# An adaLN block on one core: the work before the first scores in another order, modulation rows through SyncE's queue, x one group further ahead, slot scatters four and four, and k's two passes set between the halves of q's scaling

## Chip, core and metric

One Trainium2 chip, of which one core is used. The core has five engines with a queue of instructions each: PE (TensorE, with PEld for its weight loads), DVE (VectorE), ACT (ScalarE), POOL (GpSimd) and SP (SyncE, which only starts transfers). An engine takes its instructions in order and waits for semaphores of the others. Transfers (DMAs) are started by ACT, POOL or SP and then run by themselves. The metric is the device time of one execution in microseconds, as the median of several; smaller is better.

## What is computed

An adaptive-layernorm transformer block over 4 sequences of 2048 tokens of width 256, all in float32:

```python
mod = (silu(c) @ wmod).reshape(4, 6, 1, 256)
sa, ca, ga, sb, cb, gb = (mod[:, i] for i in range(6))
ga = (2*(ga >= 0) - 1) * maximum(abs(ga), 0.25)      # gb likewise
h = layernorm(x) * (1 + ca) + sa
x = x + ga * attention(h, w_qkv, w_out)
h = layernorm(x) * (1 + cb) + sb
x = x + gb * moe(h, w_router, w_gate, w_down)
```

The attention is causal and linear: 16 heads of 16 numbers, phi = elu + 1 on q and k, a running sum S of k v^T and z of k, out = (q S) / max(q z, 1e-6). The expert stage routes each token to 2 of 8 experts by a softmax, with a capacity of 1280 tokens an expert in the order of the tokens; all experts share the gate matrix (silu(h w_gate)) and have their own down matrix. The two weighted results are added.

## The kernel before

**Tiling.** 8192 tokens make 16 groups of 512, and a group is 4 tiles of 128. Four groups are one sequence. The kernel has two stages. The first (until about 640 us) does everything up to the routed rows, group by group; the second runs the experts over 8 × 1280 slots and adds to the output. The second stage is the same in both kernels.

**First stage.** Inside a chunk of 128 tokens the attention is done with a masked 128 × 128 score matrix per head, and across chunks with a running state. Step s of the main loop (from L876) is tile j = s mod 4 of group g = s div 4. Each step does the scores of its tile (psc, L482; masked into at, L488), the attention of the tile before (po, L545 and L558), its state and its output product (project_out, L572: pw in L576, added to x by DVE in L577, followed by the statistics of the second norm, L316). Between them stand pieces of other groups:
- g+3: load_x (L83, at j = 1, through SP) and sums (L268, row sums on ACT, at j = 3).
- g+2: deviations (L289, squares on ACT, then ve, rstd and nmr on POOL), normalise (L334, ACT), to_features (L343: transposes pta and a scaled copy hTa), and at j = 3 the two halves of k (project, L359: product pk on PE, exp into exk and relu into k on ACT; finish_keys adds them on DVE in L380 later).
- g+1: at j = 0 the two halves of q (pq, the same project), running_keys (L415: zc, a running sum of k on DVE, and qs = zc × q on POOL in L428, one half of the heads at j = 0, the other at j = 1), keys_by_token (L401: transposes of k, copied to kk), values (L382: pv, copied to vpad), denominators (L430: pd on PE, den in L441 and rden in L443 on DVE), scaled_q (L447: pr on PE, qs on DVE in L461), and at j = 3 heads_apart (L466: four scaled copies qeo on ACT).
- g−1: second norm (hrow), transposes ptm, logits (pl, L615; turned to tokens as lt, L628), ranks (L630, at j = 3), scale_rows (L596: hrow × modr on POOL in L600) and, in the next group, shift_rows (hrow + modr on DVE in L606).
- g−2: positions (L678: counts turned into places, pp), dispatch (L690: some fifteen small DVE operations L706 to L728 that make slot numbers) and send (L739): eight indirect scatters on POOL that write a group's rows into the table slots in DRAM. They are issued three at j = 2, three at j = 3 and two at j = 0 of the next group.

The order within PE, ACT, DVE and POOL is the order in which the program calls these functions. That on SP is chosen by the framework under the dependencies. In ranks, DVE takes a maximum and a difference (L644, L646), ACT the exp (gates, L647), DVE the sum sm (L649) and nine more operations to mask (L665), and POOL adds mask up into cnt (L674).

**PSUM.** pq, pk, pv, pg, pd, pw, lt, pp and the transposes take turns on three banks (pool ps); a product waits until the content of its bank has been read. Scores and po have their own.

**Lead-in.** Before the loop (L842 to L872) the pieces for group 0 and some of group 1 are called in one stretch. modulation_rows (L214) multiplies c by the columns of wmod for ga, gb (first pg), cb and sb (second pg), forms the rows on DVE (sgn, neg, then mod_rows), and sends them by ACT's queue to DRAM (mod_d, L239) and back, copied to all partitions, one transfer a sequence (modr, L241). modr's ga row is first used by gated_out (L566, POOL: wob = wout × ga), which project_out needs; its cb and sb rows by the second norm; hrow takes the gb row from mod_d (L590). constants_last (L152) sets constants of the routing. free_slots(i, then) (L731) fills one tenth of slots with a row of an unused place, by 8 SP transfers of 262 KB, and starts after the operation given. All ten must be written before the first scatter.

**x.** xpool holds 4 groups of x: load_x takes a buffer when the group it held has been written out.

Of the kernel before, what the change touches and what calls it, by code (L numbers as in the profile page):

```python
# [48 lines left out]
G = 512  # L49
NT = G // P  # L50
GPB = L // G
NH = D // P
# [14 lines left out]
def adaln_block(ctx: ExitStack, tc, x, wqkvT, woutT, wrT, wgT, wdT, cT, wmod, out):  # L67
# [3 lines left out]
    const = ctx.enter_context(tc.tile_pool(name="const", bufs=1))  # L71
    ps = ctx.enter_context(tc.tile_pool(name="ps", bufs=3, space=PSUM))
    tokens = ctx.enter_context(ExitStack())
    xpool = tokens.enter_context(tc.tile_pool(name="xpool", bufs=4))

    def bank(name):
        return ps.tile([P, 512], F32, tag="bank", name=name)
# [133 lines left out]
                modc[:, at + i].rearrange("p h b -> p (h b)"), pc[:, i * n : (i + 1) * n], float(i), None, ALU.add  # L211
            )

    def modulation_rows():  # L214

        rows_ = sp.tile([NB, 4, D], F32, name="mod_rows")
        sgn = sp.tile([NB, 2 * D], F32, name="sgn")
        neg = sp.tile([NB, 2 * D], F32, name="neg")
        for i, pair in enumerate(((2, 5), (4, 3))):
            pg = bank(f"pg_{i}")  # L220
            for n, m in enumerate(pair):
                for k in range(NH):
                    nc.tensor.matmul(
                        pg[:NB, n * D : (n + 1) * D], sc[:, k, :], wmod_sb[:, k, m * D : (m + 1) * D],
                        start=(k == 0), stop=(k == NH - 1),
                    )
            if i == 1:
                nc.vector.tensor_scalar(rows_[:, 1, :], pg[:NB, :D], 1.0, None, ALU.add)
                nc.vector.tensor_copy(rows_[:, 2, :], pg[:NB, D:])
                continue  # L230

            nc.vector.tensor_scalar(sgn, pg[:NB, :], 0.0, 2.0, ALU.is_ge, ALU.mult)
            nc.vector.tensor_scalar(neg, pg[:NB, :], -1.0, 0.25, ALU.mult, ALU.max)
            nc.vector.tensor_tensor(neg, neg, pg[:NB, :], ALU.max)  # L234
            nc.vector.scalar_tensor_tensor(
                rows_[:, 0::3, :], sgn.rearrange("b (a d) -> b a d", d=D), -1.0,
                neg.rearrange("b (a d) -> b a d", d=D), ALU.add, ALU.mult,
            )
        nc.scalar.dma_start(mod_d[:, :, :], rows_)  # L239
        for b in range(NB):  # L240
            nc.scalar.dma_start(modr[:, b], mod_d[b : b + 1, :3, :].to_broadcast([P, 3, D]))  # L241

    def token_rows():
        setup.close()
# [156 lines left out]
    def keys_by_token(g):  # L401
        kT = G_["k", g]
        kk = G_["kk", g] = w2.tile([P, NT, NH, P], F32, tag="kk", name=f"kk_{g}")
        for j in range(0, NT, 2):
            pk = bank(f"pk_{g}_{j}")
            for i in range(2):
                for h in range(NH):
                    nc.tensor.transpose(
                        pk[:, (i * NH + h) * P : (i * NH + h + 1) * P],
                        kT[:, h, (j + i) * P : (j + i + 1) * P],  # L410
                        ident,
                    )
            nc.scalar.copy(kk[:, j : j + 2].rearrange("p j h s -> p (j h s)"), pk)

    def running_keys(g, hs):  # L415

# [46 lines left out]
                pr[:, :, h, 0, :], ALU.mult,  # L463
            )

    def heads_apart(g):  # L466

        qs = G_["qs", g]
        qeo = G_["qeo", g] = w2.tile([P, NH, 2, G], F32, tag="qeo", name=f"qeo_{g}")
        for h in range(NH):  # L470
            for q in range(2):
                nc.scalar.activation(qeo[:, h, q, :], qs[:, h, :], AF.Copy, scale=par[:, q : q + 1])

# [360 lines left out]
    with tc.manual_schedule(engines={ET.PE, ET.Activation, ET.DVE, ET.Pool}):  # L834
# [35 lines left out]
        gated_out(0)  # L870
        free_slots(2, project(1, "k", 0, D, 2))
        sums(2)  # L872

        out_bank("po_first")
        last = None
        for s in range(NG * NT + 1):  # L876
# [28 lines left out]
            if tail:  # L905
# [1 line left out]
                p15a, p15b, p15c = (NG - 1, 0, 2), (NG - 1, 2, 1), (NG - 1, 3, 1)  # L907
                t = s - (NG - 1) * NT
                if t == 0:
                    send((NG - 4, 0, NT), 6, 8)  # L910
                    shift_rows(p13)
                    positions(p13)
                    done()
# [50 lines left out]
                    dispatch(p15c)  # L964
                    send(p15c, 0, 2)
            if old is not None and j in (2, 3):
                send(old, 3 * (j - 2), 3 * (j - 1))
            if s == 0:
                free_slots(3, project(1, "k", 1, D, 2))
            elif s == 2:  # L970
                modulation_columns((3, 4), 2)
                token_rows()
            if tail:
                pass
            elif j == 0:
# [8 lines left out]
                    deviations(g - 1 if prv is not None else None, nrm)  # L984
                if nxt is not None:
                    running_keys(nxt, (0,))
                if g >= 3:
                    send((g - 3, 0, NT), 6, 8)
                if old is not None:
                    shift_rows(old)  # L990
            elif j == 1:
                if nxt is not None:
                    keys_by_token(nxt)
                done()
                if old is not None:
                    positions(old)
                if nxt is not None:
                    running_keys(nxt, (1,))
                    values(nxt, 0)
                    values(nxt, 2)  # L1000
                if nrm is not None:
                    normalise((nrm, 0, NT), "a", xs[nrm], G_["xna", nrm])
                if old is not None:
                    dispatch(old)
                if far is not None:
                    load_x(far)
            elif j == 2:
                if nxt is not None:
                    denominators(nxt)
                if prv is not None:  # L1010
                    second_norm(prv)
                if nrm is not None:
                    to_features((nrm, 0, NT), "a", 0)
                done()
                if nxt is not None:
                    scaled_q(nxt)
                if prv is not None:
                    to_features(prv, "m", 2)
            else:
# [84 lines left out]
```

## Time and profile before

| | us |
|---|---|
| runs of the kernel | 948.67, 950.0, 952.56 (median 950.0) |
| profiled execution | 952.95 |
| its span, first to last instruction | 951.2 |
| busy PE / DVE / POOL / ACT | 839.8 / 553.2 / 488.5 / 417.1 |
| mean granted TensorE clock | 0.951 of full |
| first stage / second stage | about 640 / 311 |
| first scores of group 0, 1, 2, 3, 4 | 51.39, 83.34, 114.60, 156.39, 190.5 |

The last row is read from the timeline: the difference of two entries is what a group takes. In the rows of a timeline, the first number is the start in us from the span's start, the second the length of the instruction or of a run of equal ones (x and a count). Then come the engine (a q behind it means that the engine starts a transfer), the line, the operation, and output <- inputs with their shapes. A bracket gives how long the engine had stood idle before, and who ended that wait. In a table of stretches each row has the stretch, its length, the busy time of each engine with the number of instructions, the granted TensorE clock, the share of time that the transfer engines worked, and GB/s.

The two instructions with the most DVE and POOL time in the first stage are these (busy time, mean ns of one, then idle time before them): 

```profile
L488 DVE TENSOR_TENSOR at<-psc,tri 128x1024 f32<-128x1024 f32 x128 | 150.2, 1214 | 27.8 <-PE psc L482 27.8
L745 POOL DMA_INDIRECT slots<-hrow,idx x128 | 137.6, 1075 | 49.8 <-issue 35.2
```

### The profile page before, as it was taken

What the parts mean: (1) busy time and instruction counts of PE and PEld (TensorE: products, weight loads), DVE (VectorE), ACT (ScalarE), POOL (GpSimd) and SP (SyncE); (2) the same over time, 40 slices, a digit from 0 to 9 for tenths busy, and PEclk for the clock granted to TensorE, in tenths of its full rate; (3) what the DMA queues carried; (4) which work ended last, traced back from release to release, by engine and by line L of the source; (5) the groups of instructions that cost most, each with busy time, mean ns of one, the idle gap of its engine ahead of it and who ended that gap; (6) DMA issues with size and microseconds to landing.
All of it is one profiled execution on the core that took longest, in us unless ns stands there. A gap on an engine that the chain in (4) does not pass through costs nothing.

```text
span 951.2 us, 20608 instructions
## 1 busy us (share of the span) xinstructions
PE 839.8 (88%) x8234; PEld 583.2 (61%) x8234; DVE 553.2 (58%) x1193; ACT 417.1 (44%) x973; POOL 488.5 (51%) x607
## 2 busy tenths in 40 slices
PE   6599979899899889889889887628999999999995
PEld 3366656666566566566566564415767767767664
DVE  3456676797697697687687687752333333333332
ACT  3355555566566655656656533112222222222220
POOL 1321344765765676675676567651434434434334
PEclk9689999999999999999999988758999999999999
DMA  7578903313322322321221111029546546645333
GB/s 272 197 249 235 326 29 106 122 50 127 115 85 102 114 92 85 121 91 45 80 81 52 50 41 43 1 67 305 102 101 151 130 101 127 148 102 106 34 36 42
DMA packets 72217, 106.16 MB, mean 112 GB/s; under 512 B 9251, under 2 KB 44323, under 8 KB 72121
## 3 DMA queue, kind: packets, MB, share of 16 engines
q1 hardware_dynamic: 44192, 65.22, 21.4%
q0 software_dynamic: 21760, 31.99, 15.5%
q10 hardware_dynamic: 6168, 7.63, 2.3%
q8 instruction: 65, 1.06, 0.5%
q14 instruction: 32, 0.25, 0.1%
HBM read 42.97 MB, written 74.69 MB: 124 GB/s over the span
## 4 chain that ended last, share of the span: by engine, by line
PE 49%; POOL 13%; DVE 12%; issue 7%; ACT 4%; DMA 1%; POOLq 0%; another core or an unknown queue 0%; DVEq 0%; ACTq 0%; SPq 0%
PE ph L796 13%; PE pe L809 13%; PE pk L366 5%; POOL slots L745 4%; PE pw L576 3%; DVE at L488 3%; PE psc L482 2%; PE ptm L352 2%; POOL rstd L306 2%; PE pq L366 2%; PE po L558 2%; POOL qs L428 2%; PE pte L785 2%; POOL out_dram L818 1%; PE po L545 1%
## 5 line engine op out<-in xcount | busy, mean ns | idle before, releaser
L818 POOL DMA_INDIRECT out_dram<-y,tok x80 | 123.3, 1541 | 180.3 <-DVE y L814 126.4
L488 DVE TENSOR_TENSOR at<-psc,tri 128x1024 f32<-128x1024 f32 x128 | 150.2, 1214 | 27.8 <-PE psc L482 27.8
L745 POOL DMA_INDIRECT slots<-hrow,idx x128 | 137.6, 1075 | 49.8 <-issue 35.2
L796 PE MATMUL ph<-hTe,wg_sb 128*128 128x512 f32 (+1 forms) x384 | 153.1, 526 | 0.0
L809 PE MATMUL pe<-wd,hid 128*128 128x256 f32 x640 | 150.5, 379 | 0.0
L809 PEld LDWEIGHTS pe<-wd,hid 128*128 128x128 f32 x640 | 121.6, 190 | 37.0 <-issue 23.0
L802 DVE SCALAR_TENSOR_TENSOR hid<-th,ph 128x512 f32<-128x512 f32 (+1 forms) x96 | 57.4, 598 | 145.8 <-ACT th L801 140.8
L801 ACT ACTIVATE th<-ph 128x512 f32<-128x512 f32 (+1 forms) x96 | 50.5, 526 | 156.1 <-PE ph L796 153.8
L796 PEld LDWEIGHTS ph<-hTe,wg_sb 128*128 128x128 f32 x384 | 70.3, 193 | 39.0 <-issue 32.5
L482 PE MATMUL psc<-qeo,k 32*128 32x256 f32 x1024 | 75.8, 410 | 10.5 <-PE po L545 4.1
L366 PE MATMUL pk<-hTa,wqkv_sb 128*128 128x512 f32 x128 | 67.0, 649 | 6.7 <-DVE x L577 6.2
L576 PE MATMUL pw<-wob,both 128*128 128x256 f32 x236 | 65.9, 404 | 7.7 <-ACT both L513 5.4
L558 PE MATMUL po<-at,vpad 128*32 128x128 f32 x2048 | 70.8, 277 | 0.7 <-issue 0.6
L814 DVE SCALAR_TENSOR_TENSOR y<-pe,rows 128x256 f32<-128x256 f32 x80 | 38.7, 484 | 49.7 <-PE pe L809 49.7
L482 PEld LDWEIGHTS psc<-qeo,k 32*128 32x128 f32 x1024 | 48.4, 190 | 30.0 <-issue 9.4
L558 PEld LDWEIGHTS po<-at,vpad 128*32 128x32 f32 x2048 | 54.1, 110 | 18.5 <-issue 18.1
L366 PE MATMUL pq<-hTa,wqkv_sb 128*128 128x512 f32 x128 | 62.6, 614 | 0.0
L388 PE MATMUL pv<-wqkv_sb,hTa 128*128 128x256 f32 x256 | 59.9, 387 | 1.8 <-DVE neg L234 1.8
L576 PEld LDWEIGHTS pw<-wob,both 128*128 128x128 f32 x236 | 43.4, 200 | 24.2 <-issue 11.2
L788 ACT COPY hTe<-pte 128x512 f32<-128x512 f32 (+1 forms) x48 | 24.7, 514 | 69.2 <-PE pte L785 69.1
L674 POOL TENSOR_TENSOR cnt<-cnt,mask 128x8 f32<-128x8 f32 x56 | 19.5, 347 | 68.9 <-DVE mask L665 65.6
L388 PEld LDWEIGHTS pv<-wqkv_sb,hTa 128*128 128x128 f32 x256 | 47.9, 191 | 8.4 <-issue 2.3
(163 smaller groups left out, 1358.0 us busy)
## 6 DMA issues: line engine op xcount, KB each, us to landing
slots<-free SPq DMA_DIRECT2D x80, 262.0 KB, 5.2
rows<-slots SPq DMA_DIRECT2D x16, 1048.0 KB, 8.3
x<-in_x_dram SPq DMA_DIRECT2D x16, 512.0 KB
out_dram<-x SPq DMA_DIRECT2D x16, 512.0 KB, 5.6
rows<-slots SPq DMA_DIRECT2D x8, 524.0 KB, 3.6
hrow<-mod_d SPq DMA_DIRECT2D x32, 128.0 KB, 3.0
wd<-in_wdT_dram ACTq DMA_DIRECT2D x8, 512.0 KB
slots<-hrow,idx POOLq DMA_INDIRECT x128
```

Source lines behind the costliest of these rows:

```text
L366: nc.tensor.matmul(pq, wqkv_sb[:, k, o + h * P : o + (h + 1) * P], hT[:, k, :], start=(k == 0), stop=(k == NH - 1))
L388: nc.tensor.matmul(pv[:, i * D : (i + 1) * D], hT[:, k, (j + i) * P : (j + i + 1) * P], wqkv_sb[:, k, 2 * D : 3 * D], start=(k == 0), stop ...
L482: nc.tensor.matmul(psc[:, a, h], kT[r : r + 32, h, cols], qeo[r : r + 32, h, :, cols], start=True, stop=True,)
L488: masked = nc.vector.tensor_tensor(at, psc[:, 2 * m : 2 * m + 2].rearrange("p i h q t -> p (i h q) t"), tri.unsqueeze(1).to_broadcast([P, ...
L558: nc.tensor.matmul(po[32 * a : 32 * a + 32, h * P : (h + 1) * P], vp[:, j, h * 4 + a, q : q + 2, :], att[a // 2][:, a % 2, h, q, :], start ...
L576: nc.tensor.matmul(pw[:, :D], oT[:, h, :], wob[:, h, :], start=(h == 0), stop=(h == NH - 1))
L745: row = nc.gpsimd.indirect_dma_start(out=slots[:, :], out_offset=bass.IndirectOffsetOnAxis(ap=idx[:, c, j : j + 1], axis=0), in_=hr[:, j0 ...
L796: nc.tensor.matmul(ph[:, :m], wg_sb[:, k, f * P : (f + 1) * P], hTs[b][:, k, :m], start=(k == 0), stop=(k == NH - 1),)
L801: nc.scalar.activation(th[:, :m], ph[:, :m], AF.Tanh, scale=0.5)
L802: nc.vector.scalar_tensor_tensor(hids[b][:, f, :m], th[:, :m], 1.0, ph[:, :m], ALU.add, ALU.mult)
L809: nc.tensor.matmul(pe[:, :D], hids[b][:, f, j * P : (j + 1) * P], wds[e][:, f, :], start=(f == 0), stop=(f == NF - 1),)
L818: put = nc.gpsimd.indirect_dma_start(out=out[:, :], out_offset=bass.IndirectOffsetOnAxis(ap=toks[b][:, j : j + 1], axis=0), in_=y, in_offs ...
```

## The change

It has five parts.

1. **modulation_rows** becomes row_products, gate_rows and norm_rows. The rows go to mod_d in three transfers and come back in eight (four ga rows, four pairs of cb and sb rows), all by SP. In the lead-in the first half of pg stays after values(0, 0); constants_last, normalise(1) and the denominators, values, scaled_q and heads_apart of group 0 come in front of the rest; the second half of pg comes late. k's first pass and the sums that stood at the lead-in's end, and two of the slot fills, move behind the scores of step 0; gated_out(0) moves to step 0, behind running_keys(1, (0,)), which on POOL is the first half of group 1's qs.
2. **x**: five buffers, and at j = 1 of group g group g+4 is loaded, not g+3. x_3 is loaded at step 0.
3. **Scatters**: four at j = 2, four at j = 3, none at j = 0.
4. **k's passes**: at j = 3 ACT scales one half of q's heads, then does k's first pass, then scales the other half.
5. **ranks** is called in front of the output product of j = 3 and of k's second pass, not behind them.

On SP the order becomes x_0, wqkv, x_1, wg, x_2, x_3, x_4; 8 slot writes; 3 writes of mod_d; 8 broadcasts into modr; 64 slot writes; out of group 0; 8 slot writes; the 8 first gb rows of hrow; x_5. Before, it is x_0, wqkv, x_1, wg, x_2, x_3; 56 slot writes; 6 gb rows; 8 slot writes; 2 gb rows; 8 slot writes; out of group 0; 8 slot writes; x_4.

```diff
-    xpool = tokens.enter_context(tc.tile_pool(name="xpool", bufs=4))
+    xpool = tokens.enter_context(tc.tile_pool(name="xpool", bufs=5))
...
-    def modulation_rows():
+    mod_rows = sp.tile([NB, 4, D], F32, name="mod_rows")
+    def row_products(i, pair):
+        pg = bank(f"pg_{i}")
...
+        return pg
+    def gate_rows(pg):
...
-        nc.scalar.dma_start(mod_d[:, :, :], rows_)
+        for i in (0, 3):
+            nc.sync.dma_start(mod_d[:, i, :], mod_rows[:, i, :])
         for b in range(NB):
-            nc.scalar.dma_start(modr[:, b], mod_d[b : b + 1, :3, :].to_broadcast([P, 3, D]))
+            nc.sync.dma_start(modr[:, b, 0, :], mod_d[b : b + 1, 0, :].to_broadcast([P, D]))
+    def norm_rows(pg):
+        nc.vector.tensor_scalar(mod_rows[:, 1, :], pg[:NB, :D], 1.0, None, ALU.add)
+        nc.vector.tensor_copy(mod_rows[:, 2, :], pg[:NB, D:])
+        nc.sync.dma_start(mod_d[:, 1:3, :], mod_rows[:, 1:3, :])
+        for b in range(NB):
+            nc.sync.dma_start(modr[:, b, 1:3, :], mod_d[b : b + 1, 1:3, :].to_broadcast([P, 2, D]))
...
-    def heads_apart(g):
+    def heads_apart(g, hs=tuple(range(NH))):
...
         values(0, 0)
-        modulation_rows()
-        free_slots(1, denominators(0))
+        gates = row_products(0, (2, 5))
+        constants_last()
+        normalise((1, 0, NT), "a", xs[1], G_["xna", 1])
+        denominators(0)
         values(0, 2)
-        normalise((1, 0, NT), "a", xs[1], G_["xna", 1])
         scaled_q(0)
         heads_apart(0)
+        gate_rows(gates)
         to_features((1, 0, NT), "a", 0)
-        keys_by_token(0)
-        constants_last()
-        gated_out(0)
-        free_slots(2, project(1, "k", 0, D, 2))
-        sums(2)
+        norm_rows(row_products(1, (4, 3)))
+        free_slots(1, keys_by_token(0))
...
                 if t == 0:
-                    send((NG - 4, 0, NT), 6, 8)
...
             if old is not None and j in (2, 3):
-                send(old, 3 * (j - 2), 3 * (j - 1))
+                send(old, 4 * (j - 2), 4 * (j - 1))
             if s == 0:
+                free_slots(2, project(1, "k", 0, D, 2))
                 free_slots(3, project(1, "k", 1, D, 2))
+                sums(2)
+                load_x(3)
...
-                if g >= 3:
-                    send((g - 3, 0, NT), 6, 8)
                 if old is not None:
                     shift_rows(old)
+                if g == 0:
+                    gated_out(0)
...
-                if far is not None:
-                    load_x(far)
+                if g + 4 < NG:
+                    load_x(g + 4)
...
                 if nxt is not None:
-                    heads_apart(nxt)
+                    heads_apart(nxt, (0,))
                 if nrm is not None:
                     project(nrm, "k", 0, D, 2, later=True)
+                if nxt is not None:
+                    heads_apart(nxt, (1,))
                 if prv is not None:
                     logits_by_token(prv)
+                    ranks(prv)
                 done()
                 if nrm is not None:
                     project(nrm, "k", 1, D, 2, later=True)
-                if prv is not None:
-                    ranks(prv)
```

More of the change, by code (lines that the diff above doesn't have):

```diff
@@ L212, in modulation_columns @@
             )
-    def modulation_rows():
-        rows_ = sp.tile([NB, 4, D], F32, name="mod_rows")
+    mod_rows = sp.tile([NB, 4, D], F32, name="mod_rows")
+    def row_products(i, pair):
+        pg = bank(f"pg_{i}")
+        for n, m in enumerate(pair):
+            for k in range(NH):
+                nc.tensor.matmul(
+                    pg[:NB, n * D : (n + 1) * D], sc[:, k, :], wmod_sb[:, k, m * D : (m + 1) * D],
+                    start=(k == 0), stop=(k == NH - 1),
+                )
+        return pg
@@ L217, in modulation_rows @@
+    def gate_rows(pg):
         sgn = sp.tile([NB, 2 * D], F32, name="sgn")
         neg = sp.tile([NB, 2 * D], F32, name="neg")
[L219 to L238, printed above, removed]
@@ L239, in modulation_rows @@
-        nc.scalar.dma_start(mod_d[:, :, :], rows_)
-        for b in range(NB):
-            nc.scalar.dma_start(modr[:, b], mod_d[b : b + 1, :3, :].to_broadcast([P, 3, D]))
+        nc.vector.tensor_scalar(sgn, pg[:NB, :], 0.0, 2.0, ALU.is_ge, ALU.mult)
+        nc.vector.tensor_scalar(neg, pg[:NB, :], -1.0, 0.25, ALU.mult, ALU.max)
+        nc.vector.tensor_tensor(neg, neg, pg[:NB, :], ALU.max)
+        nc.vector.scalar_tensor_tensor(
+            mod_rows[:, 0::3, :], sgn.rearrange("b (a d) -> b a d", d=D), -1.0,
+            neg.rearrange("b (a d) -> b a d", d=D), ALU.add, ALU.mult,
+        )
@@ L412, in keys_by_token @@
                     )
-            nc.scalar.copy(kk[:, j : j + 2].rearrange("p j h s -> p (j h s)"), pk)
+            inst = nc.scalar.copy(kk[:, j : j + 2].rearrange("p j h s -> p (j h s)"), pk)
+        return inst
     def running_keys(g, hs):
@@ L464, in scaled_q @@
             )
-    def heads_apart(g):
+    def heads_apart(g, hs=tuple(range(NH))):
         qs = G_["qs", g]
-        qeo = G_["qeo", g] = w2.tile([P, NH, 2, G], F32, tag="qeo", name=f"qeo_{g}")
-        for h in range(NH):
+        if 0 in hs:
+            G_["qeo", g] = w2.tile([P, NH, 2, G], F32, tag="qeo", name=f"qeo_{g}")
+        qeo = G_["qeo", g]
+        for h in hs:
             for q in range(2):
```

## The prediction

> **What bounds the kernel now.** I read the page first. TensorE is busy 88% of the span, but the chain that ended last gives it only 49%; VectorE and GpSimd hold 12 to 13% each, so in places another engine sets the pace. The expert stage (640 to 951 us) has 295.5 us of TensorE work in 311 and no edit touches it. All that can move lies before. There I took the timelines engine by engine, the chain of waits, and tables by stretch.
>
> *Lead-in.* The first scores (psc) start at 51.39 us. In ScalarE's and TensorE's timelines:
>
> ```profile
> 32.04 0.52 ACTq L239 DMA_DIRECT2D mod_d<-mod_rows  x1
> 33.80 7.31 ACTq L241 DMA_DIRECT2D modr<-mod_d  x4
> 41.15 0.65 ACT L396 COPY vpad<-pv 128x256 f32<-128x256 f32 x2 [15.62 <-DMA modr<-mod_d]
> ...
> 42.35 2.79 PE L352 MATMUL pta<-ident,xna 128*128 128x128 f32 x8 [7.74 <-ACT xna L339]
> ```
>
> ScalarE stands still for 15.62 us in front of a copy whose product (pv, second half) was ready at 33.4, and normalise(1), which TensorE waits 7.74 us for, stands behind that copy.
>
> *Group 2, once.* x_4 is asked for at 115.12, behind the last slot write:
>
> ```profile
> 115.12 0.38 SPq L85 DMA_DIRECT2D x<-in_x_dram  x1
> ...
> 121.45 0.42 ACT L273 ACTIVATE xna<-x 128x256 f32<-128x256 f32 x1 [6.11 <-DMA x<-in_x_dram]
> ...
> 123.51 1.57 PE L576 MATMUL pw<-wob,both 128*128 128x256 f32 x4 [4.72 <-ACT both L513]
> 124.88 3.18 PE L366 MATMUL pq<-hTa,wqkv_sb 128*128 128x512 f32 x4
> ```
>
> The stretches by start of a group's scores (length, then busy of PE, PEld, DVE, ACT, POOL; clock; DMA) show the price and the steady period:
>
> ```profile
> 114.60:156.40 41.80, 34.44 (x451) 23.39 (x447) 27.76 (x56) 21.43 (x54) 20.04 (x29) 0.92 0.28 94
> 156.40:190.50 34.10, 31.24 (x433) 21.62 (x429) 26.73 (x56) 21.40 (x54) 22.05 (x29) 1.00 0.28 103
> 261.30:295.70 34.40, 31.52 (x448) 21.88 (x449) 26.79 (x56) 21.56 (x54) 22.72 (x31) 1.00 0.32 106
> ```
>
> *Steady state.* A period is 34.4 us with only 31.5 of TensorE. What holds it, at the end of a group (ScalarE, VectorE, TensorE):
>
> ```profile
> 290.25 2.56 ACT L472 ACTIVATE qeo<-qs,par 128x512 f32<-128x512 f32 x4
> 292.71 0.58 ACT L370 ACTIVATE exk<-pk 128x512 f32<-128x512 f32 x1
> 293.19 0.59 ACT L371 ACTIVATE k<-pk 128x512 f32<-128x512 f32 x1
> 295.22 0.60 ACT L370 ACTIVATE exk<-pk 128x512 f32<-128x512 f32 x1 [1.45 <-PE pk L366]
> ...
> 296.19 0.23 ACT L647 ACTIVATE gates<-gates 128x32 f32<-128x32 f32 x1
> ...
> 296.45 0.18 DVE L649 TENSOR_REDUCE sm<-gates 128x4 f32<-128x32 f32 x1 [2.53 <-ACT gates L647]
> ...
> 293.20 1.98 PE L366 MATMUL pk<-hTa,wqkv_sb 128*128 128x512 f32 x4 [0.52 <-DVE x L577]
> ```
>
> and earlier in it (TensorE, GpSimd):
>
> ```profile
> 281.62 0.42 PE L436 MATMUL pd<-qs,hpick 128*32 128x128 f32 x8 [1.25 <-POOL qs L428]
> ...
> 276.49 1.82 POOL L745 DMA_INDIRECT slots<-hrow,idx  x1 [0.17 <-issue]
> 278.62 0.97 POOL L745 DMA_INDIRECT slots<-hrow,idx  x1 [0.30 <-issue]
> ```
>
> From the gates' arrival (sm, 539.90) to pr (562.53) the chain of waits is 22.6 us of almost nothing but VectorE, back to back; the 11.8 us left of a period are TensorE and ScalarE up to the next gates. Two things tie for that stretch's end: this VectorE queue (rden after den) and GpSimd's qs, late behind two scatters. Removing one of the two alone gives next to nothing.
>
> **The change part by part.**
>
> *1. Lead-in.* Off ScalarE go the issues (0.52 + 7.31) and the two waits between them. [...] The row says 15.62: ScalarE's queue stays in order over a wait for the rows and one for their write. I take the row, because compute stands behind those waits, and rebuild the stretch. pg's first half (8 of 16 matmuls, half of 3.78) ends at 26.7; pd 29.0 as before; den and rden 1.2 → 30.3; second half of v to 30.9, pr 1.24 → 32.1; qs 2 × 0.6 → 33.3. ScalarE: normalise(1) 30.85 to 32.9, vpad → 33.6, qeo 2.56 → 36.1. VectorE's gate rows free pg's bank at 35.3, the other half of pg runs 35.3 to 37.1, eight transposes of k 1.1 → **38.2**, or 40.1 at half clock (the granted clock was 0.50 between 34 and 52 us). But k's first pass of group 1 (3.6 us before the first scores until now) moves behind them; at psc(0,1), where both orders have done the same, I get 47.0 to 48.9 against 58.54: 9.6 to 11.5 us, 9.6 taken.
>
> A new wait: gated_out(0) moves on GpSimd behind group 1's rstd, nmr and first qs (1.7 + 0.2 + 1.3 and their inputs). The output product pw(0,0) needs its wob: some 7.6 us after psc(0,1) where TensorE is there after 3.6, so −4.0. Queued behind pw on TensorE is all of the next step. Below: nothing, if TensorE is late itself; above: 5.7, if half clock follows (x_4's wait made pq 3.18 for 1.88). Net **−5.5** (−3.5 to −7.5).
>
> SP: its 11 modulation DMAs stand behind 8 slot writes and in front of 64. The rows land near 43, first used by group 0's second norm, far later. The 64 then run from 43.5; at 0.83 each (6.61 for 8 at 99.94) to 97, eight more and the gb rows to about 108. The first scatter is near 129. At the worst row (9.99 for 8) they end near 138, and first scatters and x_5 would lose up to 9.
>
> *2. x ahead.* x_4 is seventh on SP, in front of every slot write, so the 6.11 goes. In TensorE: 4.72 idle + (3.18 − 1.88) + (1.57 − 1.03) at low clock = **−6.6**; the two rows above differ by 7.7. x_5 now takes the place behind the writes: asked for near 108, 6.3 to land, needed near 142. Covered.
>
> *3. and 4. Scatters, k's passes.* Two scatters (0.97 + 0.30 gap each, 2.6 us) leave the front of the second qs and become the fourth ones of j = 2 and j = 3. qs was 1.25 late for pd: gone. The fourth of j = 3 stands before cnt, which waits 4.20 us for the mask; of that 1.3 goes to the scatter and 2.2 to the earlier mask, leaving 0.7 or more.
> ScalarE at j = 3: one half of qeo (1.28) → 291.53, k's first pass → 292.7, other half → 293.96, gates 0.23 → 294.2: sm starts at 294.22 for 296.45, **−2.23**. Its input (the subtraction, 293.73) comes 0.85 earlier too, as L577 and its statistics (0.42 + 0.43) go behind the ranking: they are now in the queue, **+0.85**. VectorE's stretch starts 1.38 earlier net. k's second pass loses its 0.52 wait (its bank is now the logits'), and q's second pass inherits the wait for L577, with some 2.4 us to spare.
> The fourth scatter now runs beside the ranking. [...] The row: L719 beside scatters means 380 ns over 18, against 188 for L708 of the same size, so 0.2 a meeting; one in the chain view took 1.28. I take **+0.2**, keeping 0 and +3.3 as ends.
> Per period −1.2. The next thing late is TensorE's own: 31.5 plus the 0.70 in front of psc = 32.2, against 33.2. It holds from group 1's end to group 14's, 13 periods: **−15.6**.
>
> *Tail.* It begins without two scatters (1.2 of their 2.6 stood on GpSimd's way to the second norm), and behind the same 0.85 on VectorE: 0 taken, ±1.
>
> **Sum.** 5.5 + 6.6 + 15.6 = 27.7. From the profiled execution's 952.95 (span 951.2 and 1.75 around it): 925.3. That execution is 2.95 above the median of 950.0, so **922**.
>
> **The rivals.**
> - *Only the single stalls go.* The tie hides a third: VectorE's stretch is 26.8 of 34.4 busy, and another wait (pw for a bank that den frees, 1.4 us by my count) may take all of 1.2. For it: such ties are what the profile shows in every period. Against: no engine idles between sm and pr but VectorE's suppliers. 950 − 12 = **938**.
> - *SP's queue.* Slot writes at the slow rate; scatters or x_5 up to 9 late: **931**. Against: the eight-wide batches at 0.79 to 0.87.
> - *More.* The 2.23 come through whole (13 × 2.23 = 29.0), with the lead-in's 7.5 and x's 6.6: 43.1 off 950, **907**.
> [...]
>
> **How the numbers follow.** Forecast 0.57 (914 to 930), single stalls only 0.21, SP's queue 0.06, more 0.06, slower 0.10. 908 to 942 leaves out the slower case, half of "more" and an edge of 938: about 0.17. Half a percent (4.75 us) is what a measurement can tell from none here. Faster: 0.57 + 0.06 + 0.20 + 0.05 = 0.88; same 0.04 (edges of three cases); slower 0.08.
>
> **What would show it.** Right: psc(0,0) near 38 to 40; no ScalarE row waiting for modr or x; pw(0,0) waiting 4 us for wob; no pd row waiting for GpSimd's qs; pk's 0.52 gone; gates' exp ahead of k's second pass on ScalarE, and sm right after it, some 2.2 us earlier against its group's scores; periods near 33.2. Wrong: periods still 34.4 with pw waiting longer than 1.4 (then 938), ranking operations above 0.43 in the mean (then 963), or scatters waiting on slot writes.

## The result and the profile after

| | before | after |
|---|---|---|
| median of 20 executions, us | 951.65 | 949.44 |
| lowest and highest, us | 948.67, 958.52 | 936.1, 965.5 |
| ratio | | 0.9892 [0.9866, 0.9919] |
| profiled execution, its span, us | 952.95, 951.2 | 936.1, 934.4 |
| its granted clock | 0.951 | 0.958 |

The ratio leaves out executions more than 1.5% above the fastest, and half of the changed kernel's 20 lie there. A gain of 1.1% came where 3% was forecast, and the times of one kernel lie 29 us apart. The profiled execution is the fastest of them. Its rows show first what went as planned. Lead-in (ScalarE, then TensorE):

```profile
29.36 2.07 ACT L347 ACTIVATE xna<-x,nmrm,rstdm 128x256 f32<-128x256 f32 x4 [5.31 <-POOL nmrm L339]
...
36.39 1.15 PE L493 MATMUL psc<-qeo,k 32*128 32x256 f32 x16
...
51.73 1.48 PE L587 MATMUL pw<-wob,both 128*128 128x256 f32 x4 [3.64 <-POOL wob L581]
53.00 5.25 PE L396 MATMUL pv<-wqkv_sb,hTa 128*128 128x256 f32 x16
```

The first scores come at 36.39 for 51.39, and the foreseen wait for wob is there. It costs more than itself: pv behind it takes 5.25 us instead of 3.70, with the granted clock at 0.50 from 52.89 to 56.30. In group 2 the wait for x_4 is gone, and another stall stands there, which the profile ascribes to no engine (TensorE):

```profile
117.72 1.87 PE L416 MATMUL pk<-ident,k 128*128 128x128 f32 x8 [2.78 <-issue]
119.38 1.91 PE L587 MATMUL pw<-wob,both 128*128 128x256 f32 x4
```

At the end of a steady group (ScalarE, VectorE):

```profile
279.30 1.33 ACT L483 ACTIVATE qeo<-qs,par 128x512 f32<-128x512 f32 x2
280.80 0.60 ACT L378 ACTIVATE exk<-pk 128x512 f32<-128x512 f32 x1 [0.17 <-PE pk L374]
281.29 0.59 ACT L379 ACTIVATE k<-pk 128x512 f32<-128x512 f32 x1
281.77 1.33 ACT L483 ACTIVATE qeo<-qs,par 128x512 f32<-128x512 f32 x2
283.00 0.23 ACT L658 ACTIVATE gates<-gates 128x32 f32<-128x32 f32 x1
...
283.25 0.19 DVE L660 TENSOR_REDUCE sm<-gates 128x4 f32<-128x32 f32 x1 [1.92 <-ACT gates L658]
```

The gates now stand in front of k's second pass, as built. From den to the next sm it is 11.9 us for 14.1 before (means of the eleven periods from group 3 on): the 2.2 us of the prediction. But the other part of the period, from sm to den on VectorE, has grown from 20.7 to 22.8, and nearly all is given back: the eleven groups take 34.6 us in the mean, for 34.8 before. The pages' groups of TensorE's output product and of pd show where TensorE now waits (busy, mean ns, idle before):

```profile
L587 PE MATMUL pw<-wob,both 128*128 128x256 f32 x236 | 67.4, 410 | 29.9 <-DVE den L450 24.9 <-POOL wob L581 3.6 <-ACT both L524 1.3
L445 PE MATMUL pd<-qs,hpick 128*32 128x128 f32 x256 | 10.5, 274 | 1.7 <-POOL qs L437 1.7
```

Before, 14.4 us of waits for qs stood in front of pd, and 6.2 for x in front of pk. In the steady groups both are gone, and 24.9 us of waits for den have come: one of 2.1 to 2.9 us in each period. The rows around one (TensorE, VectorE, GpSimd):

```profile
306.72 1.10 PE L587 MATMUL pw<-wob,both 128*128 128x256 f32 x4 [2.13 <-DVE den L450]
...
301.03 1.15 DVE L725 TENSOR_TENSOR gates<-gates,keep 128x32 f32<-128x32 f32 x1
...
299.17 1.24 POOL L537 TENSOR_TENSOR s_acc<-s_acc,both 128x64 f32<-128x64 f32 x1
300.48 0.37 POOL L539 TENSOR_TENSOR s_msk<-s_acc,bd 128x64 f32<-128x64 f32 x1
300.81 1.32 POOL L437 TENSOR_TENSOR qs<-zc,q 128x512 f32<-128x512 f32 x1
```

L725 is one of dispatch's small operations and took 0.19 in most periods before. Now qs, freed of the scatters, runs at its side, and it takes 1.15.

Another part of the growth belongs to this chip. In eight of the eleven stretches from sm to den VectorE waits 0.7 to 0.8 us for q, behind a pause of TensorE for which the profile shows no reason; these stretches take 23.0, the other three 22.15. One of them (TensorE, VectorE):

```profile
286.35 0.72 PE L569 MATMUL po<-at,vpad 128*32 128x128 f32 x17 [0.68 <-issue]
...
292.94 0.69 DVE L383 SCALAR_TENSOR_TENSOR q<-exq,q 128x512 f32<-128x512 f32 x1 [0.76 <-ACT q L379]
```

On the two other chips that ran the changed kernel, these waits for q are absent and the stretch from sm to den is 22.1.

### The profile page after: what moved, and what is told of

The parts are those of the page before. It is cut to its first block, busy times and chain, and to the rows that moved or that the text cites. A ratio compares the mean times of both kernels' runs of the same rounds, so it can differ in the third digit from the quotient of the medians.

```text
span 934.4 us, 20608 instructions
## 1 busy us (share of the span) xinstructions
PE 830.8 (89%) x8234; PEld 582.1 (62%) x8234; DVE 559.5 (60%) x1193; ACT 416.9 (45%) x973; POOL 482.7 (52%) x607
## 3 DMA queue, kind: packets, MB, share of 16 engines
q0 software_dynamic: 21760, 31.99, 15.6%
## 4 chain that ended last, share of the span: by engine, by line
PE 59%; DVE 23%; issue 6%; ACT 4%; POOL 4%; DMA 2%; SPq 1%; POOLq 0%; DVEq 0%; ACTq 0%
PE ph L807 13%; PE pe L820 13%; DVE at L499 7%; PE pk L374 6%; PE pw L587 5%; PE pq L374 4%; DVE zc L432 4%; PE psc L493 4%; PE po L569 4%; PE ptm L360 2%; PE po L556 2%; PE pte L796 2%; DVE hrow L617 2%; POOL out_dram L829 1%; DVE gates L725 1%
## 5 line engine op out<-in xcount | busy, mean ns | idle before, releaser
L499 DVE TENSOR_TENSOR at<-psc,tri 128x1024 f32<-128x1024 f32 x128 | 150.3, 1215 | 32.8 <-PE psc L493 29.7
L756 POOL DMA_INDIRECT slots<-hrow,idx x128 | 128.2, 1002 | 51.6 <-issue 40.8
L587 PE MATMUL pw<-wob,both 128*128 128x256 f32 x236 | 67.4, 410 | 29.9 <-DVE den L450 24.9
L569 PE MATMUL po<-at,vpad 128*32 128x128 f32 x2048 | 74.6, 275 | 6.3 <-issue 6.2
L374 PE MATMUL pk<-hTa,wqkv_sb 128*128 128x512 f32 x128 | 62.3, 612 | 0.0
L537 POOL TENSOR_TENSOR s_acc<-s_acc,both 128x64 f32<-128x64 f32 x52 | 24.9, 479 | 51.2 <-ACT both L524 39.7
```

The lines of the kernel that those rows point to most:

```text
L374: nc.tensor.matmul(pq, wqkv_sb[:, k, o + h * P : o + (h + 1) * P], hT[:, k, :], start=(k == 0), stop=(k == NH - 1))
L499: masked = nc.vector.tensor_tensor(at, psc[:, 2 * m : 2 * m + 2].rearrange("p i h q t -> p (i h q) t"), tri.unsqueeze(1).to_broadcast([P, ...
L569: nc.tensor.matmul(po[32 * a : 32 * a + 32, h * P : (h + 1) * P], vp[:, j, h * 4 + a, q : q + 2, :], att[a // 2][:, a % 2, h, q, :], start ...
L587: nc.tensor.matmul(pw[:, :D], oT[:, h, :], wob[:, h, :], start=(h == 0), stop=(h == NH - 1))
L756: row = nc.gpsimd.indirect_dma_start(out=slots[:, :], out_offset=bass.IndirectOffsetOnAxis(ap=idx[:, c, j : j + 1], axis=0), in_=hr[:, j0 ...
```

## The experiments

Each was compared with the kernel before, run beside it on the same chip; there that kernel took 941.8 to 942.8 us at the median, not 951.65, so ratios are compared and not times. In microseconds, a hundredth of the ratio is 9.4. The kernel before has no profile from these chips; where its steady groups are needed, those of only_x stand for them, which the edit of x doesn't touch (33.8 us, where 34.6 is usual in the profile of before).

| kernel | median us | ratio to before [95%] |
|---|---|---|
| only_lead | 942.51 | 0.9994 [0.9984, 1.0004] |
| only_x | 934.86 | 0.9919 [0.9897, 0.9941] |
| only_scatter | 971.61 | 1.0312 [1.0290, 1.0335] |
| only_order | 920.11 | 0.9756 [0.9743, 0.9768] |
| lead_x | 928.31 | 0.9863 [0.9845, 0.9882] |
| after_again | 931.67 | 0.9875 [0.9848, 0.9902] |
| after_third | 931.52 | 0.9871 [0.9840, 0.9901] |
| after_fill | 913.44 | 0.9694 [0.9677, 0.9712] |
| after_fill_2 | 911.86 | 0.9667 [0.9642, 0.9692] |
| scatter_fill | 951.45 | 1.0092 [1.0076, 1.0108] |
| after_33 | 905.84 | 0.9604 [0.9588, 0.9620] |
| fill_33 | 913.32 | 0.9700 [0.9687, 0.9713] |
| rows_by_act | 914.11 | 0.9705 [0.9691, 0.9719] |
| best_wob | 899.49 | 0.9558 [0.9539, 0.9577] |
| early_two | 922.66 | 0.9788 [0.9760, 0.9816] |

### The parts one by one

**only_lead**: the lead-in and gated_out's move, all else as before.

> Only the lead-in of part 1. By the trace of the changed kernel (scores of group 1 at 74.90 for 83.34) 8.4 us less than before, about 942; by the prediction's sum 5.5 less, 944.5. If the wide spread of the changed kernel's times (936 to 966) comes from the slot writes that now follow in one row, this kernel spreads by over 10 us too; if it comes from the steady groups, it stays within 4 us of its median.

It gained nothing. The scores of group 1 come at 75.11, and then group 2 takes 48.1 us. Its rows (ScalarE, SyncE, TensorE):

```profile
119.75 0.42 ACT L281 ACTIVATE xna<-x 128x256 f32<-128x256 f32 x1 [12.63 <-DMA x<-in_x_dram]
...
105.22 1.92 SPq L85 DMA_DIRECT2D x<-in_x_dram  x1
...
121.81 2.07 PE L585 MATMUL pw<-wob,both 128*128 128x256 f32 x4 [11.25 <-ACT both L522]
```

x_4 arrives near 120 whatever the lead-in does (its first use starts at 119.75 here and at 121.45 in the profile of before), so a faster lead-in only waits longer for it. The times spread by 2.8 us: the wide spread isn't from here.

**only_x**: part 2 alone.

```diff
-    xpool = tokens.enter_context(tc.tile_pool(name="xpool", bufs=4))
+    xpool = tokens.enter_context(tc.tile_pool(name="xpool", bufs=5))
...
             if s == 0:
                 free_slots(3, project(1, "k", 1, D, 2))
+                load_x(3)
...
-                if far is not None:
-                    load_x(far)
+                if g + 4 < NG:
+                    load_x(g + 4)
```

> Only x one group further ahead (x_3 loaded at step 0). If x_4's wait is worth what its rows say, 6.6 us less: 943.5. Rival: in the changed kernel group 2 is 36.97 us long and not 34.4, with a stall of 2.78 us that no engine ends; if that stall takes the place of x_4's, the gain is 4 us or less: 946 or more.

7.7 us less, a little above the 6.6 of the rows. The stall without a cause didn't show in this kernel; in its place group 2 has one wait of 3.06 us for den.

**only_scatter**: part 3 alone (send(old, 4 * (j - 2), 4 * (j - 1)), none at j = 0).

> Only the scatters four and four. By the tie as the prediction put it, next to nothing: 948 to 951, with the 1.25 us wait for qs gone and a wait of pw for den in its place. Rival: qs, now free of the scatters, meets the small operations of dispatch on VectorE, and the stretch from sm to den grows by up to 0.9 us a period: up to 962.

Neither: 29 us slower. Most steady groups take 37.4 us where only_x has 33.8. TensorE's rows, and the table of stretches for the same time (length, busy times, granted clock, DMA):

```profile
394.22 2.05 PE L576 MATMUL pw<-wob,both 128*128 128x256 f32 x4 [3.07 <-DVE den L441]
396.19 1.24 PE L454 MATMUL pr<-rden,spread 32*128 32x128 f32 x16
397.36 1.97 PE L352 MATMUL ptm<-ident,hrow 128*128 128x128 f32 x8
```

```profile
391.00:394.20 3.20, 0.15 (x2) 0.01 (x1) 3.10 (x7) 2.49 (x5) 2.08 (x3) 0.90 0.19 47
394.20:400.50 6.30, 6.28 (x48) 4.49 (x52) 2.99 (x5) 1.55 (x2) 3.29 (x5) 0.51 0.66 225
```

This is the finding of the study. With qs early, pd no longer waits, TensorE runs on to pw, and all of its idleness in the period meets in one wait of 3.1 us for den's bank. Behind it the clock is 0.51 for some 6 us: pw takes 2.05 for 1.10, pr 1.24 for 0.73, ptm 1.97 for 1.07. Ten of the eleven steady periods have low clock behind the wait; the one without takes 34.5. So some 0.7 us of a period goes with VectorE's longer stretch (21.5 for 20.7), and 1.5 to 3.2 with the clock. In the first profile of before the idleness lay in pieces (0.52, 0.41, 1.25, 0.70) with work between them. In only_x it is 0.51 in front of pk and 2.0 to 2.15 in front of pd's second half. Three of its eleven periods have slow products behind that wait too, and take 35.0 to 35.1 us. TensorE in such a period, and in one without:

```profile
305.23 0.60 PE L436 MATMUL pd<-qs,hpick 128*32 128x128 f32 x8 [1.99 <-POOL qs L428]
305.76 1.97 PE L352 MATMUL pta<-ident,xna 128*128 128x128 f32 x8
...
271.51 0.42 PE L436 MATMUL pd<-qs,hpick 128*32 128x128 f32 x8 [2.06 <-POOL qs L428]
271.87 1.09 PE L352 MATMUL pta<-ident,xna 128*128 128x128 f32 x8
```

**only_order**: parts 4 and 5 alone (k's first pass between q's halves, ranks in front).

> Only parts 4 and 5 (k's first pass between q's halves, ranks ahead). If VectorE's stretch from sm to den sets the period, its start is 2.2 us earlier and it grows by 0.8: up to 1.4 us a period, 18 in all, 932. If GpSimd's qs behind two scatters ties with it, nothing to 3 us: 947 to 951. If the wide spread of the changed kernel comes from here, the times spread by over 10 us.

22.5 us less, with a spread of 2.1: the groups take 32.3 us for 33.8. TensorE still waits for qs, but less long:

```profile
272.25 0.42 PE L436 MATMUL pd<-qs,hpick 128*32 128x128 f32 x8 [1.39 <-POOL qs L428]
```

So GpSimd's qs didn't tie; this wait grew shorter with the rest. Over the prediction's 13 periods 1.5 us each make 19.5. The rest is about what the clock took: with waits of 1.3 to 1.4 no steady period is slow, where three are in only_x, by 1.3 each.

Parts alone make 0 − 7.7 − 22.5 + 29.0 = −1.2 us; one part alone eats the other three. The whole change makes some 12 us on two other chips (next section), so the parts don't simply add.

### Is it the clock?

**after_again** and later **after_third**: the changed kernel unaltered.

> The changed kernel once more, beside its variants. Theory (low clock): one wait of TensorE for den, 2.13 us in every period, lies at the edge from which the granted clock halves for some 6 us; in an execution where it falls over the edge in part of the periods up to 3 us a period are lost. Expected: a wide spread again, over 10 us between lowest and highest, with the time rising as the mean granted clock falls. Rival (chip): the spread came from that one chip; then all within 4 us.

> The changed kernel unaltered, beside its filled twin. Theory: its executions differ in how many periods run at half clock after the wait for den, so time falls as the mean granted clock rises, and the range is over 5 us; in the profile the periods with the low clock after that wait are longer by 1 to 2.5 us than those without. Rival: all periods alike, and the times apart for another reason.

On two other chips the ratios are 0.9875 and 0.9871, with ranges of 7.4 us each: wide, though under the 10 that was expected of the first. In after_third two neighbouring groups show it in one execution (TensorE; then the table of stretches):

```profile
304.85 1.10 PE L587 MATMUL pw<-wob,both 128*128 128x256 f32 x4 [2.19 <-DVE den L450]
305.88 0.73 PE L463 MATMUL pr<-rden,spread 32*128 32x128 f32 x16
...
337.75 1.29 PE L587 MATMUL pw<-wob,both 128*128 128x256 f32 x4 [2.30 <-DVE den L450]
338.97 1.24 PE L463 MATMUL pr<-rden,spread 32*128 32x128 f32 x16
```

```profile
304.00:310.50 6.50, 5.65 (x105) 4.44 (x108) 4.78 (x8) 2.71 (x5) 5.43 (x6) 1.00 0.68 246
337.00:344.00 7.00, 6.25 (x72) 4.62 (x76) 3.88 (x8) 2.45 (x4) 4.91 (x5) 0.76 0.73 238
```

The first group took 32.8 us, the second 34.5. Of the eleven periods from group 3 on, nine have the low clock behind this wait; in after_again all eleven; in the first chip's fastest execution three.

**after_fill**, **after_fill_2** and **scatter_fill**: the transposes of pta at j = 2 are done twice, into the same bank with the same values. This adds 1.09 us of TensorE work to each group.

```diff
-            for j in range(n):
+            for j in list(range(n)) * times:
                 nc.tensor.transpose(
...
-                    to_features((nrm, 0, NT), "a", 0)
+                    to_features((nrm, 0, NT), "a", 0, 2)
```

> The changed kernel with one stage's transposes (pta) done twice at j = 2: 1.09 us more of TensorE work in front of the wait for den, which shrinks to about 1.0. Low clock: the spread falls under 5 us and the median comes to the lowest times of the changed kernel or a little under, ratio 0.98 or less, though work was added. Rival (the wait itself is the loss, not the clock): no faster than the changed kernel, or slower by up to 15 us.

> The changed kernel with the doubled transposes once more, on the chip and beside the runs of the unaltered one. Theory: no period at half clock after the wait for den, a range under 4 us, 15 us or more below the unaltered kernel. Rival: the spread stays.

> Scatters four and four alone, with the same transposes twice: the wait of 3.05 us for den becomes about 2. Low clock: the halved clock after the wait goes from most periods (2.9 us each), so 971 comes down by 15 to 35 us, ratio 0.995 to 1.015. Rival (GpSimd and VectorE block each other, TensorE only waits): no change, ratio 1.03 or more.

More work, and 18 to 20 us less time than the unaltered kernel beside it. The same place in after_fill:

```profile
296.79 1.10 PE L587 MATMUL pw<-wob,both 128*128 128x256 f32 x4 [1.34 <-DVE den L450]
297.82 0.73 PE L463 MATMUL pr<-rden,spread 32*128 32x128 f32 x16
```

The wait is 1.3 to 1.5, no period is at low clock, and the groups take 33.0. That is 18.9 us less in the eleven periods of after_again and 13.3 in those of after_third; the rest lies in group 2, whose stall is shorter, and in the last group. The range is 2.7 and 4.3 us (under 4 was expected of the second). In scatter_fill the groups come down from 37.4 to 34.65, and only three are longer, by some 1.3. It stays 0.85 above only_x: VectorE's stretch from sm to den is 21.5 there for 20.7, with L714 beside qs (L725 in the new numbering).

**after_33** and its control **fill_33**: the changed kernel with the scatters three, three and two again, without and with the doubled transposes.

> The changed kernel with the scatters three, three and two as before; all else of the change stays. If the parts add up (x 7.7 and order 22.5 on the chip that ran them alone, and the lead-in's 8 now not eaten by x_4's wait), 30 to 38 below the kernel before: ratio 0.960 to 0.968, with a spread under 5 us. Rival: the loss of the scatter part needs the old order; then the ratio stays at 0.98 or more.

> A control for the doubled transposes: added to the kernel with scatters three, three and two, where TensorE waits 1.4 us for qs in front of them and no wait of 2 us is left to shorten. Low clock: the added 1.09 us a period is a cost or is hidden, so 0 to 15 us more than without, ratio 0.960 to 0.977. Rival (doubling the transposes helps by itself): faster than without, ratio under 0.958.

Without part 3 the change gives 37 us. In this kernel, where no long wait is left, the doubled transposes cost 9 us (0.7 a group): they don't help by themselves, and the gain in after_fill is that of the clock. That both filled kernels have periods of 33.0 is chance: from sm to den and on to sm it is 22.1 + 10.9 in after_fill, where TensorE waits for den and the added work is hidden, and 21.4 + 11.6 in fill_33, where it isn't.

**early_two**: from best_wob (below), only the two scatters of j = 0 move.

```diff
                 done()
+                if g >= 3:
+                    send((g - 3, 0, NT), 6, 8)
                 if prv is not None:
                     second_moments(prv[0])
...
                     running_keys(nxt, (0,))
-                if g >= 3:
-                    send((g - 3, 0, NT), 6, 8)
```

> From best_wob (gated_out early, scatters three, three and two): only the two scatters of j = 0 move on GpSimd, from behind group g+1's first qs to in front of the second norm's ve, where GpSimd idles some 3 us. The second qs no longer waits for them. Theory (one long wait, low clock, and a small VectorE operation held by qs): the 1.4 us wait for qs goes, one wait of 2.1 us or more for den comes, the stretch from sm to den grows by 0.6, and the time rises by 8 to 25 us over best_wob: ratio 0.964 to 0.982. Rival (qs was the limit and the loss of the four-and-four scatters lay in where scatters meet the ranking): as fast or faster, ratio 0.957 or less.

22 us slower by the ratios, with the scatters at three, three and two. So it isn't four scatters beside the ranking: an early qs is enough. First best_wob, then early_two (TensorE, VectorE, GpSimd in each):

```profile
283.93 0.43 PE L445 MATMUL pd<-qs,hpick 128*32 128x128 f32 x8 [1.33 <-POOL qs L437]
...
280.37 0.19 DVE L725 TENSOR_TENSOR gates<-gates,keep 128x32 f32<-128x32 f32 x1
...
278.79 1.83 POOL L756 DMA_INDIRECT slots<-hrow,idx  x1 [0.17 <-issue]
```

```profile
361.70 2.05 PE L587 MATMUL pw<-wob,both 128*128 128x256 f32 x4 [2.25 <-DVE den L450]
...
356.11 1.15 DVE L725 TENSOR_TENSOR gates<-gates,keep 128x32 f32<-128x32 f32 x1
...
355.89 1.33 POOL L437 TENSOR_TENSOR qs<-zc,q 128x512 f32<-128x512 f32 x1
```

Beside a scatter L725 takes 0.19 us; beside qs it takes 1.15 and ends when qs ends.

### The lead-in

**lead_x**: lead-in and x, nothing else of the change.

> Lead-in and x together, scatters and steady order as before. The lead-in alone gave nothing because x_4 is asked for at the end of the slot writes, whatever comes before. With x_4 loaded early both should count: 7.7 + 8 = 15 to 16 us less, ratio 0.983 to 0.985. Rival (the lead-in's gain is lost elsewhere, at the wait for wob): ratio 0.990 to 0.992.

12.9 us less by the ratio: 5.3 more than x alone, between the two expectations. The lead-in has a worth only when x_4 doesn't wait behind it.

**rows_by_act**: after_33 with the eleven transfers of the rows issued by ScalarE at the same places (nc.sync to nc.scalar in gate_rows and norm_rows).

> The changed kernel with scatters three, three and two, but the modulation rows' eleven transfers issued by ScalarE at the same places of the program. If what counts is ScalarE standing between dependent transfers, hTa and kk come some 6 us late, and with them the first output of the running state: 3 to 6 us more than with SP, ratio 0.964 to 0.967. If the new order of the lead-in is what counts and the queue only saves issue time (1.9 to 3 us): at most 3 us more, ratio 0.961 to 0.963.

9.5 us slower than after_33 (0.9705 for 0.9604), more than either expected. ScalarE:

```profile
37.12 0.78 ACT L361 ACTIVATE hTa<-pta,modc 128x512 f32<-128x512 f32 x1 [2.88 <-DMA modr<-mod_d]
...
42.14 1.07 ACT L421 COPY kk<-pk 128x512 f32<-128x512 f32 x2 [3.57 <-issue]
```

ScalarE stands still for 6.45 us in these two places. About 4.2 of it are its own issues, which take 4.7 in all (0.82 + 1.80 + 0.27 + 1.78), and 2.2 are waits for a write of mod_d before the row can be read back. TensorE stands behind them: the scores of tile 1 come 14.6 us after those of tile 0, for 8.4. TensorE's clock is also at half for 17 us in the lead-in, for 7 in after_33; how much of the 9.5 that is, no run separates.

**best_wob**: after_33 with gated_out(0) called behind load_x(3) at step 0, in front of group 1's norm and qs.

> Scatters three, three and two as before, and gated_out(0) called right after load_x(3), in front of group 1's norm and first qs on GpSimd; else the changed kernel. If the 3.64 us wait for wob and the low clock after it (pv 5.25 for 3.70, pw 1.48 for 1.03) are a real loss, 5.6 us less than with the scatters put back alone: ratio 0.954. Rival: group 2's stall, which hangs on transfers and not on TensorE, takes it back: ratio 0.959 to 0.961.

0.9558 against 0.9604: 4.3 us, most of what was expected. wob is ready at 46.4, and the wait in front of the first pw is 0.45 instead of 3.64. This is the fastest version, 42 us below the kernel before.

## Why the prediction was wrong

**Lead-in.** The row of 15.62 was the right one to take: in rows_by_act ScalarE's queue costs 9.5 us, where its issues alone are 4.7. The first scores came at 36.39 (38.2 forecast), tile 1's at 44.79 (47.0), the wait for wob was 3.64 (4.0) with the low clock of the upper end: tile 2's scores came 13.96 later, and 8.80 in best_wob, so 5.2 us. Net with x it is 5.3, for 5.5. That is in part luck: in the profile of after group 1's scores come 8.4 us earlier than before, and not all of it reaches the end. The lead-in is worth nothing without the x part, which the prediction's sum had beside it but didn't say.

**x.** 6.6 forecast, 7.7 alone. In the profile of after group 2 still takes 36.97 us, for the new stall of 2.78.

**k's passes and ranks.** sm 2.2 earlier, 0.8 of L577 and the statistics moved behind: net 1.38 forecast, 1.5 a period measured in only_order. The size is right, but the prediction gave it only to both parts together.

**Scatters: here it failed**, in three steps. The term that fell is the −1.2 us a period, −15.6 in all. The eleven periods of the profiled execution take 34.6 us for 34.8 in the mean; those of after_third and after_again take 34.2 and 34.7, for 34.2 in only_x.

The first is the tie. The prediction said that removing one of the two (late qs, late gates) alone gives next to nothing. Earlier gates alone gain 22.5 us, and freeing qs alone costs 29: VectorE's stretch set the period, and qs didn't.

The second is the price of the new wait. The sum took TensorE's busy time as the next limit, and the rival that named the wait of pw for den, "1.4 us by my count", counted it as idle time and no more. The wait is 2.1 to 2.3 in most periods, and on two chips the clock is halved behind it in nine and eleven of eleven periods, at 1.5 us or more each. The prediction had that price (it set it on the wait for wob), but didn't ask it of a wait that comes back in every period.

The third is VectorE's stretch, summed as +1.05 a period and measured as +2.1 in the profile of after, +1.45 on the other chips. The row chosen, +0.2 where the fourth scatter runs beside the ranking, was nothing there: ahead and tie take 0.42 in both kernels. What grew is L725, beside qs: it rose by 0.96 a period, less 0.22 that L730 (L719 before) lost. The stretch is 21.4 in after_33 and 22.1 in after_fill: 0.7 us a period for a scatter that moved out of the way. Over all the profiles L725 (L714 before) starts beside a running qs 101 times. It then takes 1.14 to 1.17 us and ends 0.04 to 0.05 after qs each time. Beside a scatter it takes 0.19 each of 99 times. No run shows the +3.3 that the prediction keeps as an end for the fourth scatter: in the profile of after ahead takes 0.42 beside a scatter, and 0.42 in most groups of before, where no scatter runs beside it. Why L725 takes longer beside qs isn't shown; no run took the overlap alone away.

The profiled execution of after itself is at low clock in only three of its eleven periods. There the growth of 2.1 alone takes back the 2.2 that the order gained. Some 0.85 of it, in eight of the eleven stretches, comes with the wait for q behind TensorE's pauses, whose cause stays open.

**Sum.** With the clock kept up the changed kernel comes to 0.9694 and 0.9667, and the forecast was 922 / 950 = 0.9705. The 18 to 20 us between that and the unaltered kernel beside it are mostly the low clock. That the sum is met so closely is in part luck: the period of 33.0, for 33.2 forecast, has the 0.7 of L725 in it, and is counted from 33.8 and not from 34.4.

**Rivals.** The time looks like that of "only the single stalls go" (938 / 950 = 0.987 forecast, 0.987 to 0.989 measured), and that rival did name the wait of pw for den. But the gain of the order is whole; it is spent again. The slower case (963) asked for ranking operations above 0.43 in the mean; in the profile of after the four in ahead and tie stay at 0.39 to 0.40, and it is L725 that grew. The width of 936 to 966 on the first chip fits executions with few and with many periods at low clock: the mean granted clock falls from 0.958 in the fastest to 0.938 in the slowest. By my estimate from these figures that is some 40 us more at half clock, worth 20 us at most, so it can't be all of the 29. No execution at the low end of that clock was profiled on that chip, so this is argued, not shown.

## What to carry to other kernels

Idle time of an engine off the critical path isn't always free: in only_scatter the idleness of TensorE met in one wait of 3.1 us, the work behind it ran at a granted clock of 0.51 for 6.3 us, and 1.5 to 3.2 us of a period went with that. So where a wait is removed, ask where TensorE stands next and for how long, and whether the other engine's operations now run beside one with which they take longer, as L725 took 1.15 us beside qs and 0.19 beside a scatter. And a gain ahead of a fixed arrival time, like that of x_4, is worth nothing until the arrival is moved too.

## What the runs showed of the chip

- **Waits and the clock behind them.** Over the eleven steady groups (3 to 13) of the seventeen profiles, by the length of TensorE's wait for qs or den, this many waits are followed by low clock (granted clock under 0.9 in the next 6 us):

| wait, us | at low clock | waits |
|---|---|---|
| 1.0 to 1.6 | 2 | 88 |
| 1.6 to 2.18 | 14 | 43 |
| 2.18 to 2.5 | 28 | 41 |
| over 2.5 | 14 | 15 |

  The length alone doesn't separate them: eight waits of 2.19 to 2.28 in scatter_fill had none, and eleven of 2.20 to 2.32 in after_again all had it.
- **Steps of the clock.** In all seventeen traces the granted clock is either full or half (1.00 or 0.50), and it changes only at the edges of equal steps of 3.413 us, to within 0.002 us. The two waits of after_third shown above, each with the step that holds the most of it and the step after:

```profile
300.98:304.39 3.41, 1.68 (x44) 1.24 (x36) 3.24 (x9) 3.21 (x8) 1.74 (x3) 1.00 0.03 5
304.39:307.80 3.41, 2.95 (x36) 2.31 (x40) 3.04 (x7) 1.18 (x2) 2.74 (x3) 1.00 0.81 275
335.11:338.52 3.41, 1.11 (x8) 0.78 (x5) 3.38 (x5) 2.78 (x5) 2.36 (x3) 1.00 0.20 40
338.52:341.94 3.42, 3.42 (x26) 2.51 (x24) 2.19 (x5) 0.65 (x1) 2.18 (x3) 0.50 0.99 380
```

  The wait that ends at 304.85 is divided by an edge: TensorE is idle for 1.73 us of the step, and the clock stays at 1.00. The one that ends at 337.75 lies in one step, with 2.30 idle, and the next step is at 0.50. For the same 187 waits, by the longest idle time of TensorE in one of the steps that the wait touches: under 1.65 us, none of 115 was followed by low clock; from 1.65 to 1.95, 8 of 22; above 1.95, all 50. In these waits the idle time within one step goes with the low clock more closely than the length of the wait does. That is read from the traces alone; no run moved the edges, so the cause isn't shown.
- **A stall without an owner.** In group 2 TensorE stands 2.8 to 3.0 us in after and after_33, with "issue" as the reason and low clock behind (0.50 from 117.74 to 121.16 in after). In after_33 the transfers are busy at 98 to 100% but move only some 75 GB/s between 108 and 116 us, with the gb rows and x_5 (which takes 13.2 us to land there); and two transfers of the instruction queue end 1.5 and 0.9 us before TensorE goes on. Whether TensorE waited for instructions behind the gb rows wasn't tried.
- **Chips differ.** The same kernel before takes 951.65 us on one chip and about 942 on the three others used; in the two profiles from the first chip TensorE has pauses of 0.3 to 0.7 us marked "issue" in most groups, which the steady groups on the others lack but for one or none a run.
